# Output projection of eight head pairs as a separate seven-product stage (cross-attention and feed-forward layer, one core)

## The chip, the core and the metric

The kernel runs on one core of a Trainium2 chip. The core has a matrix engine (TensorE, PE in the profile, with its weight loads as PEld), VectorE (DVE), ScalarE (ACT), GpSimd (POOL) and SyncE (SP), which here only issues transfers. Each engine works through its own queue of instructions in the order in which they were put there, and waits at an instruction until the semaphores that it names are set. The on-chip memory is SBUF; matmul results go to the eight banks of PSUM (128 partitions x 512 fp32 values each); DRAM is reached by DMA.

The metric is the device time in microseconds; lower is better. Times are medians over runs.

## The reference

Sixteen sequences of 64 tokens with 512 features: cross-attention with 32 heads of 128, then a feed-forward part with a routed low-rank term. Shortened to what matters:

```python
q = (layernorm(x) @ Wq).reshape(b, 64, 32, 128)
k = (ctx @ Wk).reshape(b, 64, 32, 128)
v = (ctx @ Wv).reshape(b, 64, 32, 128)
score = einsum('bqhd,bkhd->bhqk', q, k) / sqrt(128) + position_bias
probs = softmax(where(mask, score, -inf))
x = x + einsum('bhqk,bkhd->bqhd', probs, v).reshape(b, 64, 4096) @ Wo
h = layernorm(x)
x = x + h @ base_W.T + base_b + lora(h, router(h))
```

All is fp32. The change concerns the product with `Wo`: a 1024 x 4096 matrix times a 4096 x 512 matrix, added to `x`.

## The kernel before, in words

**Number format.** Every large product is made from values split in two: `hi`, the value rounded to the matrix engine's fast fp32 format (a cast on ScalarE), and `lo`, the remainder (a subtraction on VectorE). The helper `split` (L69 to L71) issues both, so all casts show as L70 and all remainders as L71, told apart by their tile names. A product is then three matmuls, hi x hi, hi x lo, lo x hi (`mm3`, L256).

**Seven products for eight.** The projections to queries, keys and values divide both matrices into 2 x 2 blocks and use Winograd's form of Strassen's scheme: seven block products instead of eight, with sums of blocks before and after (`winograd`, `Queries`; the block number `i` runs in the order (1, 2, 6, 5, 7, 4, 3)). The output projection is a plain product.

**Stages.** (1) Keys and values of all heads are computed and put in DRAM (`kd`, `vd`). (2) A loop over 16 pairs of heads, `for p in range(NP)`, makes the attention. (3) The feed-forward part runs over eight tiles of 128 tokens.

**The loop.** Each iteration is written as a string of steps; a letter is one step, and the string is the order in which steps are put down. The steps are S: scores of the next pair (64 small matmuls into two banks, L470), scaled and joined with the bias `bm` on VectorE (L473), and the row maximum (L475); Q: one of seven block products of the queries of a coming pair (6 matmuls of 512 columns, L259), whose results are copied or added (`u`, `q`); P: probabilities times V for a pair (`pv_mm`, L517), whose four banks are split into `oh`, `ol`; O: one token tile of the output projection (`proj_o`: 6 matmuls of 512 columns, and one addition of the bank into `acc` on VectorE, L534); h: the end of the softmax of a head (normalise, transpose blocks, copy to `pt`, swap blocks by four small DMAs). In the middle of the loop the string is `SQQQPQQOOQOhOQOOOO`: eight O for each pair.

**What feeds it.** SP issues the loads: `kT` and `v` from DRAM, `rq` (query weights) from `wq`, `so` (output weights) from `wo`, `bm` (bias) from `fside`. GpSimd adds the mask to `bm` (L461; there are two buffers of it, one for each head of a pair, freed when VectorE's scores operation has read them) and makes the four sums of query weights that the seven products need (`s1` to `s4`, L161). ScalarE casts the weights (`gh`, `wh`), copies banks (`u`, `q21`) and does the exponentials (L481).

**Order.** Inside the loop the order on each engine is set by a scheduler that works with its own estimate of times, and by priorities and `issue_after` marks in the code. In the last part of the kernel, `with tc.manual_schedule(engines=fixed)`, the order on the named engines is that of the code.

**Buffers.** Tiles come from pools with a fixed number of buffers (`BLOCKS`, L40); a tile waits until an older one's last reader is done. The pools `raw` (10), `g` (18) and the bank pool `psp` (6) matter here.

Of the kernel before, what the change touches and what calls it, by code (L numbers as in the profile page):

```python
# [9 lines left out]
F32 = mybir.dt.float32  # L10
# [31 lines left out]
PAD = 1248  # L42
WARM = 18
# [4 lines left out]
def xattn_ffn_kernel(ctx: ExitStack, tc: tile.TileContext, x, ctxT, wq, wk, wv, wo, fside, mask,  # L48
# [56 lines left out]

    kd = [dram.tile([P, TOK], F32, tag=f"kd{h}", name=f"kd{h}") for h in range(H)]
    vd = [dram.tile([P, 2, NT, 256], F32, tag=f"vd{q}", name=f"vd{q}") for q in range(NQ)]

    with ExitStack() as actx:
        pss = actx.enter_context(tc.tile_pool(name="pss", bufs=2, space=PSUM))  # L110
        ax = ctx.enter_context(tc.tile_pool(name="ax", bufs=1))
        tp = actx.enter_context(tc.tile_pool(name="tp", bufs=1))
# [40 lines left out]
        class Weights(dict):  # L153
# [10 lines left out]
            def make(self, i):  # L164
# [7 lines left out]
                self[i] = [blk("g", f"g{c}", F32R, (P, 2, self.cols)) for c in "hl"]  # L172
# [177 lines left out]
        with tc.manual_schedule(engines={nc.tensor.engine}):  # L350
# [159 lines left out]
            def pv_mm(i, pt, v, home="o"):  # L510
                ps = [bank() for _ in range(2)]
                for t in range(NT):
                    for a in range(2):
                        r = slice(a * S, (a + 1) * S)
                        for d in range(0, P, S):
                            c = slice(i * P + d, i * P + d + S)
                            nc.tensor.matmul(ps[a][d:d + S, t * S:(t + 1) * S], lhsT=v[t // 2][r, t % 2, c],  # L517
                                             rhs=pt[r, :, t, :], start=True, stop=True)
                res = []
# [5 lines left out]
                return res  # L525

# [67 lines left out]
            w, prev, added, pts, soft, ss, ns, t = None, None, None, [], [], [], 0, 0  # L594
# [11 lines left out]

            for p in range(NP):
                steps = ("QSQQQQQQt" if p == 0 else "SQQQPQQOOQOhOQOOOO" if p + 2 < NP else
                         "SQQQPQQOQQfSeeOOOOOhh" if p + 1 < NP else "PooOOOOOOO")
                n = 0  # L610
                for c in steps:
                    if c == "P":
                        old, told = prev, t
                        prev, t = ([pv_mm(i, pts[i], v, "g" if p + 1 == NP else "o") for i in range(2)], w), 0
                        del pts[:2]
                        v = load_v(p)
                    elif c == "S":
# [5 lines left out]
                        if p == ns - 1:  # L623
                            exps_of(1)
                    elif c == "Q":
# [7 lines left out]
                        if n == 5 and p:  # L633
                            with tc.issue_after(evicted[0].ins), tc.issue_after(evicted[1].ins):
                                w = load_o(p)
# [3 lines left out]
                        if n == 7 and p + 2 == NP:  # L639
                            sar = [blk("raw", "sar", F32, (P, 2, NB)) for _ in range(2)]  # L640
                            sbw = [blk("raw", "sbw") for _ in range(KC)]
                            slb = blk("g", "slb")
                            nc.sync.dma_start(out=slb, in_=lora_b)
# [3 lines left out]
                            for kc in range(KC):  # L647
                                nc.sync.dma_start(out=sbw[kc], in_=base_wT[:, kc])
# [247 lines left out]
```

## Time and profile before

| | us |
|---|---|
| median of 3 runs | 763.17 |
| range of the runs | 762.77 to 763.19 |
| span of the profiled execution | 761.7 |

| window of the profiled execution (us) | TensorE busy | VectorE | ScalarE | GpSimd |
|---|---|---|---|---|
| 0 to 18.5: start | 16.39 | 13.10 | 11.21 | 1.80 |
| 18.5 to 325: keys and values (two windows) | 305.16 | 213.32 | 154.38 | 97.94 |
| 325 to 363: first iterations of the loop | 35.95 | 31.41 | 25.61 | 12.04 |
| 438.2 to 662.7: nine iterations | 224.50 | 174.11 | 129.69 | 48.72 |
| 716 to 761.7: feed-forward part | 42.43 | 30.48 | 17.21 | 12.93 |

The span is the time from the first to the last instruction of one execution under the profiler; the timed runs add what lies around it. A busy time is the time in which the engine had an instruction in execution; matmuls overlap, so the step from one to the next is shorter than the duration that the profile gives for one.

### The profile page before, as it was taken

What the parts mean: (1) busy time and instruction counts of PE and PEld (TensorE: products, weight loads), DVE (VectorE), ACT (ScalarE), POOL (GpSimd) and SP (SyncE); (2) the same over time, 40 slices, a digit from 0 to 9 for tenths busy, and PEclk for the clock granted to TensorE, in tenths of its full rate; (3) what the DMA queues carried; (4) which work ended last, traced back from release to release, by engine and by line L of the source; (5) the groups of instructions that cost most, each with busy time, mean ns of one, the idle gap of its engine ahead of it and who ended that gap; (6) DMA issues with size and microseconds to landing.
All of it is one profiled execution on the core that took longest, in us unless ns stands there. A gap on an engine that the chain in (4) does not pass through costs nothing.

```text
span 761.7 us, 16780 instructions
## 1 busy us (share of the span) xinstructions
PE 752.5 (99%) x6154; PEld 624.9 (82%) x6154; DVE 565.8 (74%) x1076; ACT 412.0 (54%) x1157; POOL 194.8 (26%) x271
## 2 busy tenths in 40 slices
PE   8999999999999999999999999999999999999998
PEld 6888888888788888877888888888888888888898
DVE  7986567666655776869778777787778777878975
ACT  5654444444444445667645565456645765474361
POOL 0000008108820693223220222022211232010330
PEclk9999999999999999999999999999999999999999
DMA  6685647465735446466554465436544564462011
GB/s 255 229 285 186 205 157 229 147 218 179 224 130 187 156 126 225 142 222 217 189 158 149 138 199 167 142 120 201 174 141 134 180 185 140 125 199 84 1 57 56
DMA packets 84946, 126.79 MB, mean 166 GB/s; under 512 B 11776, under 2 KB 35072, under 8 KB 84864
## 3 DMA queue, kind: packets, MB, share of 16 engines
q1 hardware_dynamic: 80624, 123.56, 49.9%
q0 software_dynamic: 4096, 2.11, 1.2%
q8 instruction: 48, 0.79, 0.5%
q14 instruction: 34, 0.28, 0.1%
q10 hardware_dynamic: 144, 0.06, 0.0%
HBM read 83.74 MB, written 35.65 MB: 157 GB/s over the span
## 4 chain that ended last, share of the span: by engine, by line
PE 91%; DVE 3%; POOL 2%; DMA 2%; issue 1%; ACT 0%; SPq 0%; DVEq 0%; ACTq 0%; POOLq 0%
PE ps L259 73%; PE yz L259 5%; PE ps L742 5%; PE ps L517 4%; PE pss L470 4%; POOL xT L333 1%; DMA cT<-in_ctxT 1%; DMA so<-in_wo 0%; DMA xT<-xb 0%; DVE bs L708 0%; DVE gl L71 0%; PE pt L104 0%; DVE s L161 0%; DVE ol L71 0%; POOL st L711 0%
## 5 line engine op out<-in xcount | busy, mean ns | idle before, releaser
L481 ACT ACTIVATE p<-p,nm 128x64 f32<-128x64 f32 x256 | 85.9, 339 | 33.3 <-DVE nm L475 31.0
L534 DVE TENSOR_TENSOR acc<-acc,ps 128x512 f32<-128x512 f32 x128 | 86.8, 681 | 21.2 <-PE ps L259 20.4
L259 PE MATMUL ps<-wh,ol 128*128 128x512 f32 x256 | 99.9, 390 | 0.8 <-DVE ol L71 0.8
L259 PE MATMUL ps<-wh,oh 128*128 128x512 f32 x256 | 100.1, 391 | 0.0
L259 PE MATMUL ps<-wl,oh 128*128 128x512 f32 x256 | 99.7, 389 | 0.0
L70 ACT CAST gh<-s 128x512 fp32r<-128x512 f32 (+1 forms) x128 | 64.4, 514 | 56.0 <-PE ps L259 45.7
L333 POOL DMA_DIRECT2D xT<-xb x128 | 69.7, 552 | 84.9 <-DVE xb L330 80.7
L71 DVE TENSOR_TENSOR gl<-s,gh 128x512 fp32r<-128x512 f32 (+1 forms) x128 | 72.0, 566 | 23.2 <-ACT gh L70 23.1
L161 POOL TENSOR_TENSOR s<-rq 128x256 f32<-128x256 f32 x32 | 25.3, 790 | 238.9 <-DMA rq<-in_wq 190.1
L71 DVE TENSOR_TENSOR ol<-ps,oh 128x512 fp32r<-128x512 f32 x64 | 39.9, 683 | 31.5 <-ACT oh L70 31.3
L70 ACT CAST gh<-raw 128x512 fp32r<-128x512 f32 x48 | 29.8, 623 | 52.8 <-PE yz L259 36.1
L259 PEld LDWEIGHTS ps<-wh,ol 128*128 128x128 f32 x256 | 48.1, 188 | 11.4 <-DVE ol L71 1.6
L259 PEld LDWEIGHTS ps<-wl,oh 128*128 128x128 f32 x256 | 48.1, 188 | 10.0
L259 PEld LDWEIGHTS ps<-wh,oh 128*128 128x128 f32 x256 | 48.0, 188 | 10.0
L71 DVE TENSOR_TENSOR gl<-raw,gh 128x512 fp32r<-128x512 f32 x48 | 35.1, 731 | 27.9 <-ACT gh L70 20.7
L461 POOL TENSOR_TENSOR bm<-bm,maskb 128x512 f32<-128x512 f32 x32 | 42.4, 1348 | 36.6 <-DMA bm<-in_fside 36.6
L481 ACT ACTIVATION_READ_ACCUMULATOR p<-p,nm 128x1 f32 x256 | 48.6, 190 | 0.0
L565 DVE TENSOR_TENSOR q<-u,ps 128x512 f32<-128x512 f32 x48 | 32.8, 683 | 20.4 <-PE ps L259 16.0
L70 ACT CAST oh<-ps 128x512 fp32r<-128x512 f32 x64 | 33.2, 590 | 11.0 <-PE ps L517 11.0
L70 ACT CAST gh<-rq 128x256 fp32r<-128x256 f32 x48 | 19.5, 406 | 36.0 <-PE ps L259 32.1
L517 PEld LDWEIGHTS ps<-pt,v 64*64 64x64 f32 x2048 | 31.9, 135 | 5.7 <-issue 5.6
L554 ACT COPY u<-ps 128x512 f32<-128x512 f32 x48 | 27.9, 581 | 15.9 <-PE ps L259 8.8
(258 smaller groups left out, 1986.2 us busy)
## 6 DMA issues: line engine op xcount, KB each, us to landing
kd<-c SPq DMA_DIRECT2D x64, 256.0 KB, 2.6
vd<-c SPq DMA_DIRECT2D x64, 256.0 KB, 2.8
kT<-kd SPq DMA_DIRECT2D x64, 256.0 KB, 3.9
v<-vd SPq DMA_DIRECT2D x64, 256.0 KB, 3.7
raw<-in_wk SPq DMA_DIRECT2D x32, 256.0 KB, 4.0
raw<-in_wv SPq DMA_DIRECT2D x32, 256.0 KB, 4.3
rq<-in_wq SPq DMA_DIRECT2D x32, 256.0 KB, 4.1
bm<-in_fside SPq DMA_DIRECT2D x32, 256.0 KB, 4.5
```

The lines of the kernel that those rows point to most:

```text
L70: first = nc.scalar.copy(hi, src)
L71: return first, (lo_eng or nc.vector).tensor_tensor(lo, src, hi.bitcast(F32), ALU.subtract)
L259: nc.tensor.matmul(o, lhsT=a, rhs=b, start=first and n == 0, stop=last and n == 2, skip_group_check=True)
L333: nc.gpsimd.dma_start(out=dst[32 * j:32 * j + 32, :, 32 * i:32 * i + 32], in_=xb[32 * i:32 * i + 32, j])
L461: nc.gpsimd.tensor_tensor(bm, bm, maskb, ALU.add)
L470: nc.tensor.matmul(ps[a * S:(a + 1) * S, t, :], lhsT=qT[n // 8][:, cq], rhs=kT[m // 8][:, ck], start=True, stop=True)
L481: nc.scalar.activation(p[:, t, :], p[:, t, :], AF.Exp, bias=nm[:, t:t + 1], accum_out=sme[:, t:t + 1])
L517: nc.tensor.matmul(ps[a][d:d + S, t * S:(t + 1) * S], lhsT=v[t // 2][r, t % 2, c], rhs=pt[r, :, t, :], start=True, stop=True)
L534: return nc.vector.tensor_tensor(acc[:, t, :], acc[:, t, :], ps, ALU.add)
L554: copy = nc.scalar.copy(s[i], b["x"])
L565: add = nc.vector.tensor_tensor(self.blocks[key], s[u], b[bk], ALU.add)
L742: nc.tensor.matmul(o, lhsT=a, rhs=b, start=start, stop=stop, skip_group_check=True)
```

## The change

Eight of the sixteen pairs, `LATER = (1, 3, 5, 7, 9, 11, 13, 14)`, are no longer projected in the loop.

- After P of such a pair, `pv_later` doesn't split the banks. It copies three of the four blocks (ScalarE), makes the four sums that the seven products need (two on VectorE, two on GpSimd) and stores all seven blocks of 128 x 512 to DRAM (`cd`), three on ScalarE's DMA queue and four on SP's.
- The loop's strings hold four O for each iteration, so that a pair that is kept is projected over two iterations. In iterations p = 3, 5, ..., 13 the string is `SwQQQPQQOQOhQOO`, where `w` loads the output weights of the kept pair; in p = 1, 2, 4, ..., 12 it is `SQQQPQQOQOhQOO`.
- The last two iterations begin the new stage: `r` loads block 1 of a kept-back pair, `W` loads two pairs' output weights, `d` splits, `D` does twelve matmuls (a chunk).
- The new stage goes through blocks 2, 6, 5, 3, 7, 4 of eight pairs. A chunk (`later_mm`) is four token tiles x three matmuls of 256 columns. Loads are issued eight chunks ahead and splits four chunks ahead. After a block the banks are added into `acc` (`later_add`). Between the chunks stand the eight O of the last pair, the splits of the feed-forward weights (`ffn_weights`, before in the loop) and the first norms. The order of VectorE is fixed here, too.
- High and low part of the query weights' splits share a tile in pool `g`, and tiles of the feed-forward part come from `g`.

```diff
+    def later_mm(banks, s, m, first, last):
+        (sh, sl), (mh, ml) = s, m
+        for t in range(4):
+            o = banks[t // 2][:, 256 * (t % 2):256 * (t % 2 + 1)]
+            for n, (a, b) in enumerate(((sh, mh), (sl, mh), (sh, ml))):
+                nc.tensor.matmul(o, lhsT=a[:, t * P:(t + 1) * P], rhs=b, start=first and n == 0 and t % 2 == 0,
+                                 stop=last and n == 2, skip_group_check=True)
...
+            def pv_later(p, pts, v):
+
+                (b00, b01), (b10, b11) = [pv_banks(i, pts[i], v) for i in range(2)]
+                a11, a12, a22, s1, s2, s3, s4 = (blk("g", n) for n in ("a11", "a12", "a22", "s1", "s2", "s3", "s4"))
+                with tc.high_priority(offset=SOON):
+                    nc.scalar.copy(a11, b00)
+                    nc.vector.tensor_tensor(s3, a11, b01, ALU.subtract)
+                    nc.scalar.copy(a22, b11)
+                    nc.vector.tensor_tensor(s1, b01, a22, ALU.add)
+                    nc.scalar.copy(a12, b10)
+                    nc.gpsimd.tensor_tensor(s2, s1, a11, ALU.subtract)
+                    nc.gpsimd.tensor_tensor(s4, a12, s2, ALU.subtract)
+                for i, a in ((1, a11), (7, s3), (4, a22), (5, s1), (2, a12), (6, s2), (3, s4)):
+                    (nc.scalar if i in (1, 2, 4) else nc.sync).dma_start(out=cd[p][:, i - 1], in_=a)
...
+            def first_ops(n):
+
+                if n % 2 == 0:
+                    made[:] = [blk("g", f"th{c}", F32R, (P, 2, 256)) for c in "hl"]
+                    split(made[0], made[1], wr[n // 2][0][:, :, 0:256])
+                a = raws.pop(0)
+                sh, sl = [blk("g", f"sh{c}", F32R) for c in "hl"]
+                split(sh, sl, a)
+                ready.append(((sh, sl), [m[:, n % 2] for m in made]))
...
-                steps = ("QSQQQQQQt" if p == 0 else "SQQQPQQOOQOhOQOOOO" if p + 2 < NP else
-                         "SQQQPQQOQQfSeeOOOOOhh" if p + 1 < NP else "PooOOOOOOO")
+                steps = ("QSQQQQQQt" if p == 0 else "SQQQPQQOQOhQOO" if p % 2 == 0 and p + 2 < NP or p == 1 else
+                         "SwQQQPQQOQOhQOO" if p + 2 < NP else "SQrrQrrQWPQWQOrrrWdQWdvQdfSeeDOdDOhDOh" if p + 1 < NP else
+                         "ddPDrdDDdDw")
...
                     if c == "P":
-                        old, told = prev, t
-                        prev, t = ([pv_mm(i, pts[i], v, "g" if p + 1 == NP else "o") for i in range(2)], w), 0
+                        if p - 1 in LATER:
+                            pv_later(p - 1, pts, v)
+                        else:
+                            prev, t = ([pv_mm(i, pts[i], v) for i in range(2)], w), 0
...
+                    elif c == "w":
+                        w = load_o(p - 1 if p + 1 < NP else p)
...
-                        if n == 5 and p:
-                            with tc.issue_after(evicted[0].ins), tc.issue_after(evicted[1].ins):
-                                w = load_o(p)
...
+    AHEAD = 4
+    order = [(i, n) for i in (2, 6, 5, 3, 7, 4) for n in range(NL)]
+    order.insert(3, (1, NL - 1))
+    fixed = {nc.gpsimd.engine, nc.tensor.engine, nc.scalar.engine, nc.vector.engine}
+    given = {(1, NL - 1): ready.pop(0)}
     with tc.manual_schedule(engines=fixed):
...
+        for k in range(-2 * AHEAD, len(order)):
+            for ahead, f in ((2 * AHEAD, later_load), (AHEAD, later_ops)):
+                if 0 <= k + ahead < len(order) and order[k + ahead] != (1, NL - 1):
+                    f(*order[k + ahead])
+            if k < 0:
+                continue
+            i, n = order[k]
+            own = i in (2, 5, 3)
+            if own and n == 0:
+                ys = [bank() for _ in range(2)]
+            later_mm(ys if own else xs, *given.pop((i, n)), own and n == 0, n == NL - 1)
+            if n == NL - 1:
+                for half, col in {1: [(0, 0)], 2: [(0, 0)], 6: [(0, 1)], 5: [(0, 1), (1, 1)], 3: [(0, 1)],
+                                  7: [(1, 1)], 4: [(1, 0)]}[i]:
+                    later_add(ys if own else xs, half, col)
+            if i == 2 and n >= 4:
+                proj_o(n - 4, *prev)
+            if i in (6, 5) and n % 2:
+                ffn_weights(n // 2 if i == 6 else 4 + n // 2)
+            if i == 7:
+                if n < 4:
+                    ffn_norm(n)
...
+                if n == NL - 1:
+                    for t in range(4, NT):
+                        proj_o(t, *prev)
...
```

`later_load` reads one block of one pair from `cd`; `later_ops` splits it, and for every second pair also makes and splits the matching block of the output weights (`later_turn`, whose differences are made on GpSimd).

## The prediction

> **What bounds the kernel now.** I read the page first (busy shares), then the chain of waits, then one period of the attention loop engine by engine, then the matmuls by form.
>
> ```profile
> PE 752.5 (99%) x6154; PEld 624.9 (82%) x6154; DVE 565.8 (74%) x1076; ACT 412.0 (54%) x1157; POOL 194.8 (26%) x271
> ```
>
> TensorE is busy for 99% of the span, and the chain of waits runs through it almost everywhere. One period of the loop, in the chain (start, length, what):
>
> ```profile
> 587.84 2.02 PE pss L470 x64
> 589.86 4.32 PE ps L259 x18
> 594.18 2.04 PE ps L517 x128
> 596.22 16.56 PE ps L259 x72
> 612.78 2.02 PE pss L470 x64
> ...
> 678.08 0.70 DVE q L565
> ...
> 719.13 1.41 PE ps L742 x12
> ```
>
> A pair takes 612.78 - 587.84 = 24.94 us: scores 2.02, 18 query matmuls, probabilities times V 2.04, then 72 matmuls (24 of queries, 48 of the output projection) with nothing between them. One 128x512 matmul costs 4.32 / 18 = 0.24 where the pace changes and 0.2267 in a long run (13.60 us for 60, elsewhere in the chain). Twelve matmuls with 256 columns (L742) took 1.41, so 0.1175 each. Waits of TensorE are few; one of 0.70 stands before the last scores.
>
> What the other engines do in that period (timeline), and how long the bias loads take (the bias tile's own view):
>
> ```profile
> 589.75 0.33 SPq L460 DMA_DIRECT2D bm<-in_fside  x1
> ...
> 593.64 0.74 POOL L161 TENSOR_TENSOR s<-rq 128x256 f32<-128x256 f32 x1 [19.75 <-DVE q L565]
> ...
> 595.31 2.07 ACT L70 CAST oh<-ps 128x512 fp32r<-128x512 f32 x4 [0.45 <-PE ps L517]
> ...
> 595.93 2.48 DVE L71 TENSOR_TENSOR ol<-ps,oh 128x512 fp32r<-128x512 f32 x4 [2.33 <-ACT oh L70]
> ...
> 596.53 2.57 POOL L461 TENSOR_TENSOR bm<-bm,maskb 128x512 f32<-128x512 f32 x2
> ```
>
> ```profile
> L461 POOL TENSOR_TENSOR bm<-bm,maskb x4: 1297/1310/1752, 596.5 to 624.0; 128x512 f32<-128x512 f32 x4
> ...
> DMA to landing us min/median/max: 4.0/4.4/5.6
> ```
>
> The reader is to see an order: GpSimd makes the four weight sums s first and adds the mask to the bias bm afterwards; ScalarE casts the four oh in one block as soon as P ends. In a row, one cast of oh costs 2.07 / 4 = 0.52 and one remainder ol 2.48 / 4 = 0.62. The window of this period shows VectorE busy for 19.30 of 24.94 us, ScalarE 14.45, GpSimd 5.38.
>
> **TensorE's work.** Removed: 8 pairs x 48 = 384 matmuls of 512 columns, 384 x 0.2267 = 87.1 us. Added: 8 x 7 x 12 = 672 of 256 columns, 672 x 0.1175 = 79.0. Net -8.1. (With half of a 512-column step, 0.1133, it would be -10.9; I take the row that has the shape.) The built program's counts are these: 768 projection matmuls become 384, and 672 stand on the new line; all others are the same in number.
>
> A rule speaks against this. The Trainium skill, "TensorE: Matmul & The Clock Gate", Part 3 (Packing small matmuls), says that a weight load overlaps running matmuls only if it goes to another row group; its section on LDWEIGHTS gives 107 ns for 128 columns. These matmuls use all rows, so by the rule 256 columns would cost an estimated 0.107 + 0.109 = 0.216, 512 columns 0.32, and the net would be 145 - 123 = +22 us. The trace has 0.1175 and 0.2267 with a load for each matmul, so here the loads are hidden, and the sum goes by the rows.
>
> **Other engines in the loop.** Per two pairs TensorE now needs 2 x (66 x 0.2267 + 4.06) = 38.0 us instead of 49.9. VectorE loses 8 sums into acc, 4 remainders ol and 2 remainders wl (14 x 0.62 to 0.68, some 9 us) and gets s3 and s1 (1.3): 2 x 19.3 - 7.8 = 31 of 38 us, 81% instead of 77%. ScalarE swaps four casts for three copies and gets three DMA issues on its queue (SP's take 0.33 to 0.45 each): about 28 of 38. GpSimd gets two sums of 1.31: 13.4. Traffic: 56 blocks of 262 KB written and read, 29 MB on top of 126.8; the loop stays under the 255 GB/s of the first slices. By shares all of this is hidden under TensorE; only order can hurt.
>
> **Order.** I compared the order of instructions in the two built programs. Iterations alternate: in L the pair just finished goes to DRAM, in N (p = 3, 5, 7, 9, 11, 13) it is kept and cast to oh, ol. In N, ScalarE's queue now reads:
>
> ```
> gq<-rq, gq<-rq, oh, gq<-s2 [waits GpSimd], oh, gq<-s1, gq<-s3 [waits GpSimd], gq<-rq, oh, gq<-s4, oh, u
> ```
>
> and GpSimd's reads bm, bm, s1, s2, s3, s4: reversed against the row above. The third oh (second head, first half of the tokens) is what the first projection of N needs in its second half. Offsets from the first scores matmul of N:
> - VectorE. Its last operations of L, from the second sum into acc (TensorE delivers at 14.9 of 19.0): acc, rc, gq, rc, gq, q, p, acc, pb, gq, acc, four gq = 0.62 + 0.2 + 0.4 + 0.15 + 0.4 + 0.62 + 0.66 + 0.62 + 0.7 + 0.4 + 0.62 + 1.6 = 7.0, to 21.9 of L = 2.9 of N. Then the two scores operations, done at 3.6 and 4.2. They free the two bias buffers.
> - Bias loads issue then and land 4.4 later: 8.0, 8.6. GpSimd: bm 9.3, 10.6; s1 11.4, s2 12.1 (0.75 each).
> - ScalarE: gq<-s2 12.5 (0.355), oh 13.0, three gq 14.1, oh 14.6; VectorE's ol 15.2.
> - TensorE reaches that second half at 2.02 + 18 x 0.2267 + 2.04 + 12 x 0.2267 + 3 x 0.2267 = 11.5.
>
> So TensorE waits 3.7 us in each N. Queued behind the held casts are the copy u, which the next query block needs (done at 16.0, just when it is wanted), and the second head's exponentials, which have an iteration of slack. Lower bound: VectorE has no backlog (scores operations done at 1.7 and 2.3, as at 589.0 to 591.0 of the old period) and loads take the least, 4.0: s2 at 9.8, third ol at 12.9, wait 1.4. Upper: loads at 5.6: 4.9. I take 3.0, below the hand result, because the backlog is the least sure part: 6 x 3.0 = 18.0 (8 to 29). L has no cast behind GpSimd. There the stores of s1, s2 and s4 stand in SP's queue and wait for VectorE (10.0) and GpSimd (two sums of 1.31, 12.7); behind them are the last v load, wanted in the next P, and the swaps of pt, whose copy is ready at 15. So they cost nothing; if GpSimd were over 2 us later, pt would be late for P next. The three stores on ScalarE's queue stand before the copy u of L, wanted after a projection at 12.2 and done at 11.5.
>
> **The passage to the new stage.** After the last scores VectorE has, in one queue, the softmax of the last two pairs and the split operands of the first block product. Counting from the last q (0): scores operation of head 30 done at 5.6, its maximum at 7.5 and that of head 31 at 10.1, exponentials on ScalarE (0.334 each) to 12.9, then rc, rc, p, th, pb, sh to 15.9. TensorE wants that sh (fifth chunk) at 14.0: 1.9. The seventh chunk waits 0.4; the first of the next block 1.5, behind two ol; a later one 0.35. Together 4.2, call it 4.5 (1.5 to 7). The 0.70 shown above stays.
>
> **The new stage itself.** Eight chunks take TensorE 96 x 0.1175 = 11.3. VectorE: 12 remainders x 0.62 = 7.4, plus in the worst block (i = 5) four sums and four remainders of the feed-forward weights moved here, 12.4. The lead of four chunks (5.6 us) covers the 1.1. In i = 7 norms and sums make 13.3, covered by four projections (5.4). The cover fails if GpSimd's differences slow VectorE: wl<-so took 968 ns on average, 0.3 more than the 0.69 of undisturbed ones; 16 differences would cost 4. I take 0.5 (0 to 4), and 0.5 (0 to 2) for the shorter first iteration, where VectorE is already busy for 31.4 of 38 us. Loads from DRAM are issued eight chunks ahead, 5.6 us before their cast, against 3.9 for kT<-kd: hidden. The feed-forward part keeps its matmuls.
>
> **Sum** on the profiled execution: 761.7 - 8.1 + 18.0 + 4.5 + 0.5 + 0.5 = 777.1. The runs' median is 763.17, 1.5 above the span: 778.6.
>
> **Rivals.**
> - The queues don't hold (faster): bias or weight sums are there before the casts, so only the passage remains: 763.2 - 8.1 + 4.5 = 759.6, and 755 if that is hidden too. For: the old loop ran with no wait at 77% VectorE. Against: the bias buffer is freed only by N's own scores, and 4.0 us is the shortest landing seen. It decides if all new waits together stay under 8.1 us, that is under 0.6 per N with the passage as priced. Chance 0.20.
> - New waits just equal the saving: 763. Chance 0.05.
> - VectorE bounds the new stage (each block at 12 remainders at 0.97, or 11.6 against 11.3, before any sum) on top of the waits: 6 blocks x 2 to 3 more, 792. For: the slowed rows. Against: they are slow only beside GpSimd. Chance 0.10.
> - The forecast, 766 to 790 by itself (all bounds at one end would be 765 and 797): 0.65.
>
> About 0.2% is what a measurement here tells from no change. So faster 0.20, same 0.05, slower 0.75. The range reaches into the fast rival: 758 to 791, with about 0.1 left on each side.
>
> **What would show it.** In the profile after: TensorE idle before L275 (the projection), put down to ol, some 3 us in every second period; ScalarE's gq waiting for GpSimd's s, and GpSimd's first bm in N starting near 8 us after the scores; periods of about 19 and 22 us in turn; 672 matmuls at 0.1175. Wrong if N and L are equally long, or if ol is ready with P's end; then the time is near 760. If the stage between attention and the feed-forward part takes well over 90 us, VectorE bounds it.

## The result: 822 us in place of 763

The changed kernel took 822.12 us (median of 4 runs, 818.39 to 825.92) against 763.18 (762.77 to 763.55) for the kernel before on the same chip: a ratio of 1.0755, 95% interval 1.071 to 1.080, slower. The direction was as predicted, the size was not: 778.6 with a range of 758 to 791. The profiled execution of the changed kernel has a span of 824.1 us against 761.7.

The first view of the profile after, as before: busy time and share of each engine, and below it TensorE's granted clock, one digit for each fortieth of the span (9 stands for 0.9 and more).

```profile
PE 775.4 (94%) x6442; PEld 650.7 (79%) x6442; DVE 571.5 (69%) x1081; ACT 443.3 (54%) x1218; POOL 240.9 (29%) x303
...
PEclk9999999999999999999999999999998988999999
```

TensorE was to get 8.1 us less work. It was busy for 22.9 us longer (775.4 against 752.5) and idle for 48.7 in place of 9.2. More busy time for less work means a slower clock: its mean was 0.969 here and 0.999 before.

The chain of waits shows one L period and one N period (start, length, what):

```profile
495.89 2.02 PE pss L486 x64
497.91 4.10 PE ps L275 x18
502.01 5.60 DMA kT<-kd
...
507.69 0.33 ACTq L560
...
508.06 0.59 ACT u L589
...
508.69 7.09 PE ps L275 x30
515.79 2.02 PE pss L486 x64
517.80 2.68 PE ps L275 x11
520.48 4.22 DMA rq<-in_wq
...
526.36 0.75 POOL s L173
...
527.13 0.41 ACT gq L71
...
528.84 0.59 ACT oh L71
529.43 0.02 issue
529.46 0.70 DVE ol L72
530.16 0.04 issue
530.21 9.25 PE ps L275 x32
539.45 2.02 PE pss L486 x64
```

Before, this view had TensorE in every line of such a period. In N (515.79 to 539.45, 23.66 us) it now runs over the load of the raw query weights, GpSimd's sum s, the cast gq that waits for s, the casts oh queued behind it on ScalarE, and the remainder ol, before TensorE goes on. From s on this is the predicted chain; at its head stands the load rq, where the prediction had GpSimd's addition of the bias (bm). GpSimd's timeline in the N of p = 3 shows it (the bracket is the idle time before, and what ended it):

```profile
389.07 2.52 POOL L477 TENSOR_TENSOR bm<-bm,maskb 128x512 f32<-128x512 f32 x2 [13.95 <-DMA bm<-in_fside]
393.12 0.74 POOL L173 TENSOR_TENSOR s<-rq 128x256 f32<-128x256 f32 x1 [1.53 <-DMA rq<-in_wq]
```

In all six N the first sum begins 0.13 to 0.18 us after the second rq load has landed, and in five of them GpSimd had been idle for 0.5 to 1.5 us since bm. SP issues rq behind the bias loads here (387.10 after 386.00); in the kernel before it was issued ahead of them (588.50 before 589.75).

In the L of the chain above (19.90 us) a store on ScalarE's queue (ACTq L560) waits for a kT load, and the copy u behind it comes late. The last 32 matmuls of N take 9.25 us; at 0.2267 each they would take 7.25.

Where such 2 us come from shows in another N (p = 7), in windows (from:to, length, busy time and instruction count of PE, PEld, DVE, ACT, POOL, then the granted clock, the DMA share and GB/s):

```profile
471.40:485.50 14.10, 12.28 (x226) 9.83 (x225) 8.24 (x16) 8.56 (x30) 5.82 (x6) 1.00 0.79 246
485.50:487.50 2.00, 1.27 (x3) 0.86 (x4) 1.42 (x3) 2.00 (x7) 0.00 (x0) 0.82 0.51 191
487.50:489.50 2.00, 2.00 (x7) 1.52 (x6) 2.00 (x7) 2.00 (x13) 0.00 (x0) 0.50 0.00 0
489.50:491.50 2.00, 2.00 (x9) 1.64 (x8) 1.53 (x3) 1.09 (x5) 0.00 (x0) 0.83 0.30 85
491.50:495.80 4.30, 4.30 (x20) 3.30 (x18) 3.75 (x9) 0.39 (x1) 0.00 (x0) 1.00 0.17 52
```

TensorE waits in this N for 0.62, 1.70 and 0.23 us between 482.7 and 486.7. Right after, while it is fully busy, the clock stands at 0.50 for some 3 us. A wait in N is paid a second time in slow matmuls.

**Where the 70.5 us are.** The matmul counts alone make the profiled execution 761.7 - 8.1 = 753.6. The starts of the scores matmuls (L470 before, L486 after) cut both traces into stretches. The third column is the stretch before with its matmuls removed or added: in the loop 4 projections of 6 matmuls, 24 x 0.2267 = 5.44; after the last scores 12 projections less and 79.0 more.

| stretch | before | matmuls alone | after | over | predicted |
|---|---|---|---|---|---|
| start to the scores of pair 1, then p = 1 | 335.2 + 27.9 | 335.2 + 22.5 | 336.6 + 25.9 | 4.8 | 0.5 |
| six L (p = 2, 4, ..., 12) | 149.8 | 117.2 | 121.9 | 4.7 | 0 |
| six N (p = 3, 5, ..., 13) | 149.6 | 117.0 | 146.7 | 29.7 | 18.0 |
| p = 14 to the last scores | 15.4 | 15.4 | 19.3 | 3.9 | 0 |
| last scores to the end | 83.8 | 146.4 | 173.7 | 27.3 | 5.0 |

In the six N TensorE was busy for 132.1 us where 117.0 would do: 15.1 of the 29.7 are slow matmuls, 14.6 are idle time. The profiled execution is the slowest of the four timed ones (825.92 us); the stretches are those of this one execution.

### The profile page after: what moved, and what is told of

It reads as the page before. It is cut to its first block, busy times and chain, and to the rows that moved or that the text cites. A ratio compares the mean times of both kernels' runs of the same rounds, so it can differ in the third digit from the quotient of the medians.

```text
span 824.1 us, 17715 instructions
## 1 busy us (share of the span) xinstructions
PE 775.4 (94%) x6442; PEld 650.7 (79%) x6442; DVE 571.5 (69%) x1081; ACT 443.3 (54%) x1218; POOL 240.9 (29%) x303
## 4 chain that ended last, share of the span: by engine, by line
PE 68%; DMA 10%; DVE 7%; ACT 5%; issue 4%; POOL 4%; SPq 1%; ACTq 0%; DVEq 0%; POOLq 0%
PE ps L275 48%; PE ps L114 7%; PE yz L275 5%; PE ps L857 4%; PE pss L486 3%; DMA kT<-kd 3%; DMA v<-vd 2%; POOL xT L349 2%; DMA wr<-in_wo 2%; ACT p L497 2%; DMA rq<-in_wq 1%; DVE shl L72 1%; ACT u L589 1%; PE ps L533 1%; DVE wl L72 1%
## 5 line engine op out<-in xcount | busy, mean ns | idle before, releaser
L114 PE MATMUL ps<-th,shh 128*128 128x256 f32 x384 | 76.1, 296 | 6.6 <-ACT shh L71 4.4
L114 PEld LDWEIGHTS ps<-th,shh 128*128 128x128 f32 x384 | 64.7, 204 | 7.5 <-ACT shh L71 7.4
L275 PE MATMUL ps<-wh,oh 128*128 128x512 f32 x128 | 52.6, 411 | 13.4 <-ACT oh L71 11.9
L72 DVE TENSOR_TENSOR gl<-s,gh 128x512 fp32r<-128x512 f32 x64 | 45.8, 721 | 21.4 <-ACT gh L71 21.1
L114 PE MATMUL ps<-th,shl 128*128 128x256 f32 x192 | 57.2, 298 | 2.3 <-DVE shl L72 2.3
L275 PE MATMUL ps<-wh,ol 128*128 128x512 f32 x128 | 52.4, 409 | 1.1 <-DVE ol L72 1.1
L71 ACT CAST gh<-s 128x512 fp32r<-128x512 f32 x64 | 39.7, 623 | 24.8 <-PE ps L275 16.2
L275 PE MATMUL ps<-wl,oh 128*128 128x512 f32 x128 | 51.5, 402 | 0.0
L569 DVE TENSOR_TENSOR acc<-acc,ps 128x512 f32<-128x512 f32 x64 | 43.0, 675 | 8.2 <-PE ps L275 8.0
L533 PEld LDWEIGHTS ps<-pt,v 64*64 64x64 f32 x2048 | 33.2, 137 | 13.0 <-issue 12.3
L533 PE MATMUL ps<-pt,v 64*64 64x64 f32 x2048 | 35.8, 223 | 7.2 <-DMA pt<-pb 6.3
```

What stands on the lines that cost most here:

```text
L71: first = nc.scalar.copy(hi, src)
L72: return first, (lo_eng or nc.vector).tensor_tensor(lo, src, hi.bitcast(F32), ALU.subtract)
L114: nc.tensor.matmul(o, lhsT=a[:, t * P:(t + 1) * P], rhs=b, start=first and n == 0 and t % 2 == 0, stop=last and n == 2, skip_group_check=True)
L275: nc.tensor.matmul(o, lhsT=a, rhs=b, start=first and n == 0, stop=last and n == 2, skip_group_check=True)
L569: return nc.vector.tensor_tensor(acc[:, t, :], acc[:, t, :], ps, ALU.add)
```

## The experiments

Each was timed in 3 rounds beside the kernel before. The runs of one kernel lie up to 1.1% apart, so a difference under 4 us between two medians is no finding by the times alone; the stretches of the traces are given with it.

### The order in ScalarE's queue: casts_last

```diff
-                            with tc.issue_after(nxt.last):
+                            with tc.issue_after(nxt.last), tc.issue_after(nxt.third if p % 2 and p > 1 else nxt.first):
                                 pairs[p + 2] = Queries(load_pair(p + 2), ORDER)
```

> Only the place of the seven weight casts gq in ScalarE's queue is changed, in the iterations p = 3, 5, ..., 13: they stand behind the third u copy, and so behind all four oh, instead of between them. Theory A (the queue holds the oh copies back behind a cast that waits for GpSimd, and the waits then halve TensorE's clock): the N iterations go from 24.5 us to 19.0 to 20.0, the time falls by 27 to 33 us, to 789 to 795 (ratio 1.034 to 1.042), and the waits of TensorE for oh (11.9 us) and for u (8.1 us) nearly vanish. Theory B (the queue holds, but the half clock has another cause that stays): only 3.7 us per iteration come back, 22 us, so 800 (1.048), with granted clock near 0.97 as before. Theory C (the added work itself, not its order: VectorE, ScalarE and the DMA engines have too much in these iterations): below 5 us, 817 to 826.

797.32 us, ratio 1.0407 [1.0366, 1.0449]. The N periods became 19.5, 19.5, 19.5, 20.5, 20.3 and 19.4 us, together 1.7 over the matmuls alone in place of 29.7. TensorE's waits after p = 0 (what waited, for what; sum in us, times, longest):

```profile
PE ps L275 <- ACT u L589: 8.3, 3, 3.7
PE ps L533 <- DMA pt<-pb: 6.3, 1, 6.3
PE ps L114 <- ACT shh L71: 5.2, 2, 3.7
...
PE ps L275 <- issue: 1.6, 2, 1.1
```

The wait for oh (11.9 us in the changed kernel) is gone from the list, and the clock is 1.00 in every N. No instruction was added or removed: 28 of the 29.7 us were the place of seven casts in a queue. Theory A holds for N, and C falls. The time itself, 24.8 us less by the medians, lies between the ranges of A (27 to 33) and B (22), and against A the waits for u did not vanish: the three that are left, 8.3 us, are those of p = 1 (3.7), p = 12 and p = 14. What halves the clock is the next run's question.

### The clock: filled_wait

```diff
                 for i, ct in enumerate(cts):
+                    if fill and i:
+                        idle = small_bank("pss")
+                        for _ in range(fill):
+                            nc.tensor.matmul(idle[:, 0:256], lhsT=zero[:, 0:P], rhs=zero, start=True, stop=True)
                     mm3(ps, [a[:, c] for a in ct[b]], w[i], i == 0, i == 1)
...
-                        added = proj_o(t, *prev)
+                        added = proj_o(t, *prev, fill=16 if t == 0 and 1 < p < NP - 1 else 0)
```

> Added: 16 matmuls of zeros (128x256, bf16) between the two halves of the first output block of p = 3, 5, ..., 13, where TensorE sits idle for 1.7 us at p = 7. Nothing else moves; nothing is added to the result. Theory A (the wait is what halves the clock some 0.7 us later): the wait is filled, the clock stays at 1.00 in all six iterations, each gets shorter by 1.5 to 1.9 us, the time falls by 8 to 12 us, to 810 to 814 (ratio 1.062 to 1.067), although TensorE has 10 us more to do. Theory B (the half clock comes from something else, or from waits that are left, 0.6 and 0.2 us): the time stays within 818 to 826, or rises by up to 3 us where the fill is longer than the wait; half clock still seen after each first block.

The N of p = 5 as a window, first of the changed kernel, then of this one (columns as above):

```profile
427.30:451.10 23.80, 21.85 (x261) 17.04 (x260) 17.73 (x36) 14.10 (x51) 5.37 (x6) 0.93 0.55 178
```

```profile
426.30:449.10 22.80, 21.60 (x275) 17.56 (x274) 16.13 (x36) 14.01 (x51) 5.40 (x6) 1.00 0.57 184
```

With 16 matmuls more TensorE is busy for less time, because the clock stays at 1.00; it did in all six N, and they took 134.6 us together in place of 146.7. So in N the wait is what halves the clock, and filling it saves the second payment: A is right about the mechanism. The whole gained less: 818.59 us, 1.0691 [1.0651, 1.0731], 3.5 below the changed kernel where 8 to 12 were expected. In the profiled execution one L (449.1 to 473.3) took 24.2 us with a wait for u and a clock of 0.67 behind it, which gave back 4.

### The passage: swaps_first, half_parts, stores_on_sync, passage_order

From the last scores to the end of attention the changed kernel's TensorE waits at these places (the bracket is the idle time before the instruction and what ended it), and SP issues this:

```profile
669.24 2.33 PE L533 MATMUL ps<-pt,v 64*64 64x64 f32 x64 [6.32 <-DMA pt<-pb]
683.76 0.38 PE L114 MATMUL ps<-th,shh 128*128 128x256 f32 x1 [2.90 <-ACT shh L71]
685.82 0.58 PE L114 MATMUL ps<-th,shl 128*128 128x256 f32 x1 [1.68 <-DVE shl L72]
```

```profile
655.93 4.07 SPq L662 DMA_DIRECT2D wr<-in_wo  x8
660.04 3.74 SPq L681 DMA_DIRECT2D v<-vd  x4
664.13 9.28 SPq L521 DMA_DIRECT2D pt<-pb  x12
```

The swaps of pt, whose copy was ready at 655.6, stand behind twelve loads in SP's queue. swaps_first turns that order round:

```diff
-"SQrrQrrQWPQWQOrrrWdQWdvQdfSeeDOdDOhDOh"
+"SQrrQrrQWPQWQOrrrdQdQdfWvWSeeDOdDOhDOh"
...
-                        load_wr()
+                        with tc.issue_after(swapped[-1].ins) if len(wr) > 1 else ExitStack():
+                            load_wr()
```

> In p = 14 the loads of the third and fourth part of Wo for the new stage (8 DMAs of 256 KB) and of the last values (4 DMAs) are put behind the pt swaps of pair 14's second head in SP's queue, instead of ahead of them. Theory A (the swaps stood 8.5 us behind these loads in one queue, and TensorE waited 6.3 us for them, then ran at a clock of 0.59): the wait goes, the time falls by 7 to 10 us, to 812 to 815 (ratio 1.064 to 1.068). Theory B (the DMA engines themselves are full, 0.85 to 0.97 of them busy in these 40 us, so that what is put last comes late instead): the swaps land sooner but TensorE waits for the casts of wr or for the final values in their place; 0 to 3 us, 819 to 822, or slower.

823.8 us, 1.0744 [1.0688, 1.08]: nothing gained, theory B. The wait for pt was gone, and others had come in its place:

```profile
674.57 0.38 PE L114 MATMUL ps<-thh,shh 128*128 128x256 f32 x1 [2.74 <-ACT shh L71]
...
687.93 0.58 PE L114 MATMUL ps<-th,shh 128*128 128x256 f32 x1 [7.46 <-ACT shh L71]
```

Is it then the number of bytes? half_parts leaves 2 MB of loads out, on top of casts_last.

```diff
                 n = len(wr)
+                if n > 1:
+                    wr.append(wr[n - 2])
+                    return
```

> On top of casts_last (797.3): the third and fourth part of Wo for the new stage are not loaded (8 DMAs of 256 KB, 2 of the some 16 MB moved between 637 and 700 us); the first and second part stand in for them, so all other instructions stay. swaps_first moved these loads and gained nothing. Theory A (the passage is bound by what the DMA engines can carry, 300 to 400 GB/s): 2 MB less at 0.25 to 0.4 MB per us are 5 to 8 us, with half clock after the waits up to 10: 787 to 792 (ratio 1.031 to 1.038). Theory B (the passage is bound by a chain that the loads only stand beside: scores, softmax, swaps, P, the store of pair 14 and its reload): 0 to 3 us, 794 to 798.

795.24, 1.0395 [1.0351, 1.044]. The wait for pt went from 6.3 to none, the waits for shh and shl of this stretch grew, and the second block began 30.2 us after the last scores in place of 34.2; the rest took 141.0 in place of 139.6. The time is in B's range (794 to 798).

stores_on_sync takes up what ended the wait for u in p = 14: ScalarE held by its own store.

```diff
-                    (nc.scalar if i in (1, 2, 4) else nc.sync).dma_start(out=cd[p][:, i - 1], in_=a)
+                    nc.sync.dma_start(out=cd[p][:, i - 1], in_=a)
```

> On top of casts_last (797.3): the three stores of a11, a22 and a12 in each L iteration are issued from SP's queue instead of ScalarE's. Theory A (a store on ScalarE's queue waits for the transfer eight issues earlier, so ScalarE's copies a and u behind it come late; seen as ScalarE waiting 3.1 us for a transfer of wr in p = 14, and as TensorE waiting for u): the 3.2 us of p = 14 and the 1.4 us of p = 12 go, 3 to 6 us less with their half clock: 791 to 794 (ratio 1.036). Theory B (the wait only changes place: SP's queue is held instead and the swaps of pt come later): 0, or up to 6 us slower, with TensorE waiting for pt.

798.37, 1.0443 [1.0398, 1.0487]. The six L took 118.4 us in place of 121.9, with no wait for u left in them, and p = 14 went from 18.9 to 17.3 (in kernels that don't move all three stores it lies anywhere between 17.5 and 20.7). But pt came late: TensorE waited 0.6 to 1.0 us for it in three N, and 7.7 in place of 6.3 after the last scores. B, the wait changed its place.

passage_order puts several of these together, and moves the casts of p = 1 (`p % 2` without `and p > 1`). It has the edit of swaps_first too; `newest` holds the last sr load issued so far.

```diff
-                    (nc.scalar if i in (1, 2, 4) else nc.sync).dma_start(out=cd[p][:, i - 1], in_=a)
+                    (nc.scalar if i in (1, 2, 4) else nc.gpsimd if p == 14 and i in (3, 6) else nc.sync).dma_start(out=cd[p][:, i - 1], in_=a)
...
-                ffn_weights(n // 2 if i == 6 else 4 + n // 2)
+                with tc.issue_after(newest[-1].ins):
+                    if i == 6 and n == 1:
+                        nc.sync.dma_start(out=bb, in_=base_b.partition_broadcast(P))
+                    ffn_weights(n // 2 if i == 6 else 4 + n // 2)
```

> On top of casts_last (797.3), with the casts of p = 1 moved in the same way, and in the passage an order in SP's queue by when TensorE wants things: pt swaps of pair 14 before the third and fourth part of Wo, the s2 and s4 of pair 14 stored from GpSimd's own queue, the sr loads before those of the feed-forward weights. p = 1 alone: 25.9 to 21 or 22 us, so 792. Theory A (the passage loses its time by the order in queues): from the last scores to the end 173.8 becomes 161 to 166; the time 779 to 786 (ratio 1.020 to 1.030). Theory B (the passage is one chain: P of pair 14, its store, its reload, and VectorE's remainders, slowed beside GpSimd): 171 or more, the time 789 to 794.

798.5, 1.0452 [1.0414, 1.0489]. p = 1 did as expected, 20.6 us in place of 25.9, in this run and in all later ones with its casts moved. The passage gained 2.5 us up to the second block, and 5.3 were lost behind it: 176.6 from the last scores to the end, against 173.8 in casts_last. That is theory B's sign (171 or more), but the time is above B's 789 to 794 too: the new order itself cost something behind the second block.

### VectorE beside GpSimd: diffs_early, casts_and_diffs, no_differences, diffs_on_vector

The weights of the new stage need sixteen differences on GpSimd (L749). In the changed kernel they run from 679.4 on, and this is VectorE's timeline beside them:

```profile
683.39 0.68 DVE L72 TENSOR_TENSOR ol<-ps,oh 128x512 fp32r<-128x512 f32 x1
683.99 3.46 DVE L72 TENSOR_TENSOR shl<-sr,shh 128x512 fp32r<-128x512 f32 x2
...
692.45 1.78 DVE L72 TENSOR_TENSOR th<-wr,th 128x512 fp32r<-128x512 f32 x1
694.15 1.78 DVE L72 TENSOR_TENSOR shl<-sr,shh 128x512 fp32r<-128x512 f32 x1
696.62 0.69 DVE L72 TENSOR_TENSOR shl<-sr,shh 128x512 fp32r<-128x512 f32 x1 [0.69 <-ACT shh L71]
```

The ol that reads PSUM keeps its 0.68 us; remainders of the same size with both operands in SBUF take up to 1.78. diffs_early makes the last eight differences sooner, with six buffers for td (`TDAT` is 5):

```diff
+            if i == TDAT and n % 2 == 0:
+                later_td(7, n // 2)
+            if i == 3 and n % 2:
+                later_td(4, n // 2)
```

> The eight differences td for the last two blocks of the new stage are made by GpSimd during the blocks i = 5 and i = 3, when it is idle, instead of between the norms of the FFN in GpSimd's queue (6 buffers for td instead of 2). Theory A (late td behind the power operations delays the casts, the remainders and with them VectorE's adds that free the banks): TensorE's waits of 1.5, 0.4 and 2.2 us in 750 to 766 go, and with them the half clock after them (0.81, 0.79): 5 to 8 us less, 814 to 817 (ratio 1.067 to 1.071). Theory B (VectorE's load bounds this stretch, 7.2 of 8 us busy in most windows): under 2 us, 820 to 824.

816.39, 1.0657 [1.0601, 1.0713]: within theory A's range, and in its trace the waits behind 750 are gone. Together with casts_last:

> casts_last and diffs_early together, nothing else. Theory A (their waits lie in different stages and add up): 797.3 less 6 to 8, 789 to 792 (ratio 1.031 to 1.035). Theory B (the early differences only move work ahead of what the passage then waits for): 794 to 798.

795.91, 1.0411 [1.0363, 1.0459]: theory B, nothing beside casts_last's 797.3. The waits of 750 to 766 were gone, but a new one of 4.78 us for an acc sum stood at 680: GpSimd, with nothing to wait for, ran the differences in one block from 656.7 on, and VectorE was slow for that much longer. So what diffs_early gained (168.4 us from the last scores to the end in its trace, 173.7 in the changed kernel's) did not come again. no_differences takes the cause away: the parts of Wo are cast without the differences.

```diff
-            r = later.tile([P, 2, 256], F32, tag=tag, name=tag, bufs=n)
-            nc.gpsimd.tensor_tensor(r, x, y, ALU.subtract)
-            return r
+            return x
```

> On top of casts_last (797.3), with the casts of p = 1 moved too (p = 1 alone: 792): GpSimd's sixteen differences of Wo's parts are left out and the parts themselves are cast instead; all else stays. Theory A (VectorE's remainders take 1.2 to 1.8 us beside GpSimd's differences, 0.68 without, and this is what makes TensorE wait for shl and acc between 655 and 740): all VectorE rows of the stage at 0.69, TensorE's waits for acc (2.1), shh (1.5) and shl (2.5) of the stage gone, 6 to 10 us with their half clock: 782 to 786 (ratio 1.025 to 1.030). Theory B (VectorE's rows are slow but off the path): 0 to 2 us, 790 to 793.

782.68, 1.0257 [1.0212, 1.0303]. From the last scores to the end 164.1 us in place of 173.8, and TensorE without a wait from 660 to 740: within theory A's range. VectorE's remainders in the stage (busy time, mean ns), casts_last from 660 to 755 us first, then no_differences from 655 to 745:

```profile
L72 DVE TENSOR_TENSOR shl<-sr,shh 128x512 fp32r<-128x512 f32 x46 | 35.1, 774 | 4.4 <-ACT shh L71 4.1
...
L72 DVE TENSOR_TENSOR th<-wr,th 128x512 fp32r<-128x512 f32 x7 | 7.5, 1066 | 0.0
L72 DVE TENSOR_TENSOR th<-td,th 128x512 fp32r<-128x512 f32 x8 | 5.9, 739 | 5.8 <-ACT th L71 5.8
L72 DVE TENSOR_TENSOR th<-t,th 128x512 fp32r<-128x512 f32 x8 | 5.5, 685 | 0.0
```

```profile
L72 DVE TENSOR_TENSOR shl<-sr,shh 128x512 fp32r<-128x512 f32 x45 | 30.5, 688 | 8.5 <-ACT shh L71 7.4 <-PE ps L114 0.7
L72 DVE TENSOR_TENSOR th<-wr,th 128x512 fp32r<-128x512 f32 x22 | 16.2, 736 | 0.5 <-ACT th L71 0.5
```

So 9.7 us from the last scores to the end are the price of GpSimd's differences. How they are paid is shown only in part. VectorE needs 54.0 us for 69 remainders with them and 46.7 for 67 without, some 6 us more for the same number (an estimate from these rows). But no_differences also takes away the waiting for the differences themselves: in casts_last ScalarE's casts th waited 8.2 us for td, and VectorE 5.8 behind them. The two were not separated. diffs_on_vector then lets VectorE make them (`nc.vector` for `nc.gpsimd` in the line above).

> casts_last with the casts of p = 1 moved too, and the sixteen differences of Wo's parts made by VectorE instead of GpSimd. Theory A (GpSimd slows VectorE more than the differences cost VectorE itself: 16 x 0.69 = 11 us, in a stage where it was busy for 94 of 120 us without them): no row of the stage above 0.8 us, 783 to 788 (ratio 1.026 to 1.032), against 782.7 with the differences left out and 792 with them on GpSimd. Theory B (VectorE becomes the bound of the stage): 790 or more, with TensorE waiting for shl all through it.

793.54, 1.0366 [1.0328, 1.0405]; 172.5 us from the last scores to the end. shl ran at 687 ns, and the 11 us of VectorE's own time cost 8.4. Theory B by the time, though TensorE's waits in the stage come to 3.7 us between 706 and 735, not all through it. The stage has no room for this work on either engine.

### What is left of the passage: both_and_less, passage_filled, loads_ahead, loads_ahead_bare

both_and_less joins no_differences, half_parts and the queue orders of passage_order but for the swaps.

> no_differences, and in the passage the third and fourth part of Wo not loaded (the first and second stand in), s2 and s4 of pair 14 stored from GpSimd's queue, sr loads before the feed-forward weights. If queue order, transfers and GpSimd beside VectorE together are what the passage and the new stage lose, the time from the last scores to the end goes from 173.8 to 148 to 155 (146.4 is what the matmuls alone make it by the counts), and the whole to 769 to 777 (ratio 1.007 to 1.017). If the chain of pair 14 through its store and reload bounds the passage on its own, it stays at 160 or more and the time above 781.

783.67, 1.0262 [1.0227, 1.0298], 166.3 from the last scores to the end: the second case, and no better than no_differences alone.

passage_filled adds zero matmuls before P of pair 14 and before the second block, to diffs_on_vector.

```diff
+                        if p + 1 == NP:
+                            filled(small_bank("pss"), 52)
...
+                if i == 2:
+                    filled(psf.tile([P, D], F32, tag="pt", name="pt"), 30)
```

> diffs_on_vector, with matmuls of zeros in TensorE's queue where it waits in the passage: 52 before P of pair 14 (52 x 0.107 = 5.6 us, the wait was 5.75) and 30 before the second block (3.2, the wait was 3.7). Theory A (what the passage loses beside its waits is the half clock that follows them, 6.9 us of TensorE's time between 616 and 660 in no_differences): clock 1.00 through the passage, 4 to 7 us less than diffs_on_vector (777 to 783, ratio 1.018 to 1.025), with waits no shorter than 1 us in all. Theory B (the passage is bound by its chain, so that a faster TensorE only waits longer): within 2 us of diffs_on_vector.

790.93, 1.0343 [1.0298, 1.0388]. The clock was 1.00 through the passage but for 635 to 645 (0.80 and 0.86), where diffs_on_vector, without the fill, has 0.50 to 0.86 in four windows of 5 us; but the stretch from the last scores to the end went from 172.5 to 173.4: TensorE, no longer slow, waited for pt again (2.4 us behind the fill). That is theory B, although the median is 2.6 us lower, which is no finding: unlike in N, a faster TensorE only arrives earlier.

loads_ahead gives the first three loads of the second block buffers of their own, before the last swaps; loads_ahead_bare does so without the differences.

```diff
+                        for tag, n in (("t4l", 2), ("t3l", 1)):
+                            both = tp.tile([P, n, D], F32, tag=tag, name="sr")
+                            for k in range(n):
+                                with tc.issue_after(swapped[-1].ins):
+                                    nc.sync.dma_start(out=both[:, k], in_=cd[LATER[len(early)]][:, 1])
+                                early.append(both[:, k])
```

> diffs_on_vector (793.5), with pair 14's swaps ahead of the third and fourth part of Wo, s2 and s4 of pair 14 stored from GpSimd's queue, and the first three sr loads of the second block in free token tiles, issued before the swaps of pair 15. Theory A (what is left of the passage is the wait for the pt swaps and then for sr, whose buffer came free late): both waits under 1.5 us, the time from the last scores to the end 172.5 becomes 162 to 166, the time 783 to 788 (ratio 1.024 to 1.031). Theory B (VectorE's operands for the first block's chunks bound the passage, since the projections that covered the softmax are gone): waits for shl and shh of the first block take their place, 790 to 794.

> loads_ahead with the sixteen differences left out (the parts themselves are cast). Theory A: as no_differences (782.7, 164.1 from the last scores to the end), less 6 to 10 us: 773 to 777 (ratio 1.012 to 1.017). Theory B: within 3 us of 782.7; TensorE's idle time between the last scores and the second block stays 8 us or more.

794.45, 1.0381 [1.032, 1.0443], and 784.04, 1.0266 [1.0221, 1.031]: theory B in both by the time. In the second, all three loads had been issued by 634, and the second block still waited:

```profile
635.98 0.39 PE L114 MATMUL ps<-thh,shh 128*128 128x256 f32 x1 [2.46 <-ACT shh L71]
...
649.78 0.58 PE L114 MATMUL ps<-th,shh 128*128 128x256 f32 x1 [4.89 <-DVE ol L72]
```

ScalarE's queue shows why (start, length, what, and in the bracket what it waited for):

```profile
643.37 1.07 ACT L71 CAST oh<-ps 128x512 fp32r<-128x512 f32 x2 [7.45 <-PE ps L533]
646.58 0.62 ACT L71 CAST shh<-a 128x512 fp32r<-128x512 f32 x1 [2.14 <-DMA a<-cd]
...
649.10 1.14 ACT L71 CAST shh<-sr 128x512 fp32r<-128x512 f32 x2
```

The loads sr of the second block have landed by 639.7 and are cast last, behind the oh of the last P and behind pair 14's block, which is written to DRAM and read back. ScalarE was idle for 7.45 us before that, so the order of its queue is a rival here as it was in N: a version with these casts ahead of oh was not tried. All kernels beside each other (us; the matmuls alone are 64 scores at 2.02, 18 projection matmuls, 84 of 256 columns and two P at 2.04, in sum 20.1, and 146.4 - 20.1 = 126.3):

| kernel | last scores to second block | second block to end |
|---|---|---|
| matmuls alone | 20.1 | 126.3 |
| changed kernel | 33.4 | 140.3 |
| filled_wait | 33.6 | 140.2 |
| diffs_early | 33.3 | 135.1 |
| casts_last | 34.2 | 139.6 |
| swaps_first | 35.2 | 139.7 |
| half_parts | 30.2 | 141.0 |
| stores_on_sync | 37.3 | 141.4 |
| casts_and_diffs | 34.6 | 139.7 |
| passage_order | 31.7 | 144.9 |
| no_differences | 33.2 | 130.9 |
| both_and_less | 31.1 | 135.2 |
| diffs_on_vector | 34.6 | 137.9 |
| passage_filled | 36.6 | 136.8 |
| loads_ahead | 37.6 | 137.8 |
| loads_ahead_bare | 35.5 | 130.0 |

In the right column GpSimd's differences are 8.7 of the 13.3 us that casts_last is over (9.7 between passage_order and both_and_less, of which the second also leaves loads out). The two kernels that load sr ahead of the feed-forward weights are 4 to 5 us worse there than their neighbours; why was not looked into. The left column is open. It loses 10 to 17.5 us in every kernel (8.9 of passage_filled's 16.5 are the fill), whichever wait was taken away, so taking away one wait was never enough; that it is the run through P, store, reload, casts and P again, for want of the projections that used to cover it, fits all runs but was not shown by removing that run as a whole. A pair 14 that is not stored at all was not tried. No version beat the kernel before: of those that leave nothing out passage_filled comes nearest, 3.4% above it.

## Why the prediction was wrong, step by step

- **What bounds the kernel, and the matmuls.** Right. The 256-column matmuls came at three in 0.36 us in the stage, 0.12 each for the 0.1175 taken, 1.7 us over all 672, each with its weight load. The rule of the Trainium skill that the prediction set aside ("TensorE: Matmul & The Clock Gate", Part 3), by which they would have been an estimated 0.216, does not hold here in the wording that the prediction took from it; the same part also lets a load be pulled ahead when it goes to the background weight buffer, and the prediction left that out.
- **The N iterations, 6 x 3.0 = 18.0.** Right was that the casts oh stand in ScalarE's queue behind a cast that waits for GpSimd (casts_last); the idle time was 14.6 us, within the bounds of 8 to 29 and close to the 18.0. The step that failed is the price of a wait: the sum had no term for what it does to the matmuls behind it, and these cost 15.1 us at a lower clock, as much again as the waits. A second step was wrong without changing the sum: what makes GpSimd late. The working put the sums s behind the addition of the bias, and left out that SP now issues rq behind the bias loads; in five of the six N GpSimd had done bm and waited for rq. At p = 7 the hand schedule had bm end at 9.3 and 10.6 and s2 at 12.1 after the scores, the trace has the second bm ending at 10.0 and s2 at 12.2: that the times agree so well is in part luck. casts_last removed both the waits and the slow matmuls, filled_wait the slow matmuls alone. The words "L has no cast behind GpSimd" stand; the waits were put down to oh, not to ol.
- **The list of N.** It began at p = 3. The iteration of p = 1 also casts four oh with gq among them, so it was a seventh N: 5.3 us by moving its casts, against 0.5 for the whole first iteration.
- **"The three stores on ScalarE's queue stand before the copy u of L ... done at 11.5."** Wrong. The third store is held by a transfer issued earlier (kT in L, wr in p = 14), and u with it. In the profiled execution TensorE waited for u for 0.7, 0.5, 0.1 and 1.1 us in four L and for 2.1 in p = 14; the rest of the 4.7 in L is 0.2 to 0.3 of busy time in each and one gap of 0.8. Moving the stores took the waits out of L and gained nothing in the whole, because SP's queue then held pt.
- **The passage, 4.5.** 13.3 us up to the second block, and 3.9 before it in p = 14. The working followed VectorE's queue and left out SP's. The loads that the change adds (16 of Wo, 8 of first blocks, the last values) were costed by bytes only, and the swaps that had to pass them were not seen. Correcting that order alone, however, gained nothing; the step that failed is the assumption that the passage is a sum of waits. In every run another wait came in place of one that was taken away, as in a chain with hardly any slack; which links bound it stays open.
- **The new stage, 0.5 (0 to 4).** 14.0 behind the second block's start. The row that told it was read (wl<-so at 968 ns) and the price taken from it, 4 us for sixteen differences, was put at the upper bound; measured, it is 8.7 to 9.7. The rival in which VectorE bounds the new stage, 792 at 0.10, came nearest to this; its argument against, that the rows are slow only beside GpSimd, was the case here, for the differences run beside them.

## What to carry to other kernels

Price a new wait of a busy TensorE of some 1.5 us or more at up to twice its length: once idle, and, where the clock drops, once more in the matmuls behind it (15.1 beside 14.6 us in the six N; after the last scores 10.9 beside 16.4). Then ask first whether the order of an in-order queue, not the work, makes it. Work taken out of a loop as "moved" was also the cover for something; list what it covered (here the last softmax, its swaps and the reload) before pricing the place it moves to. Where two waits are found in one stretch, remove both in one run before believing in either.

## What the runs showed of the hardware

- Waits of 0.62, 1.70 and 0.23 us within 4 us put the granted clock to 0.50 for some 3 us of full work (windows of p = 7), and matmuls of zeros in the gap kept it at 1.00 in all six N. Not every such wait does it: 2.00 us in diffs_early (p = 3) and 3.20 in casts_last (p = 14) left it at 1.00. From 338 us on, every wait of 3.3 us or more in these traces was followed by about 0.50 within 4 us. The Trainium skill, "TensorE: Matmul & The Clock Gate", section "HAM oscillation — how this bites in real kernels", puts the limit at idle gaps of about 3.4 us; here waits half as long, with a few matmuls between them, were often enough.
- A remainder of 128x512 on VectorE took 0.68 us alone and up to 1.78 while GpSimd subtracted, and 0.68 beside it when it read PSUM. The Trainium skill, "SBUF — State Buffer", section "SBUF: two separate sides", says that VectorE with two SBUF inputs and GpSimd lock the same pair of ports for a whole instruction; this trace agrees.
- In the kernels with the casts moved, TensorE idled for 0.3 to 1.5 us with nothing to wait for ("issue") at up to four places some 20 us apart (in casts_last at 490.6, 510.4, 530.9 and 551.2 us). The changed kernel has one such gap (0.8 at 548.6), the kernel before none. The cause is open.
